# Four edits to the end of a conv-attention, additive-attention and expert kernel: residual and gate loads, the weight buffers, and the last chunk's attention

## The chip, the core and the metric

The kernel runs on one core of one Trainium2 chip. Times are microseconds (us) of the device; the metric is the median of the runs of the whole kernel. Five engines work side by side and wait for one another by semaphores: PE (TensorE, matmuls and transposes), DVE (VectorE), ACT (ScalarE), POOL (GpSimd) and SP (SyncE), which in this kernel issues every DMA.

## What is computed

Eight images of 128 channels and 36 x 36 = 1296 pixels pass through two layers, all in float32.

```
# layer 0, on the group-normed image: 1x1 conv, convolved queries, keys, values, attention, two 1x1 convs
x = x + conv_attention(group_norm(x))
t = tokens(x)                                   # (8, 1296, 128)
# layer 1a: additive attention
y = layer_norm(t);  q = y @ Wq.T + bq;  k = y @ Wk.T + bk
s[b,i,j] = sum_d w[d] * tanh(q[b,i,d] + k[b,j,d]) + bw
t = t + softmax_j(s) @ y
# layer 1b: 64 experts, each takes the 8 tokens of an image with the largest gate
y = layer_norm(t);  p = softmax over the tokens of (y @ gate_w.T + gate_b)     # (8, 1296, 64)
topv, topi = 8 largest of p along the tokens, for each image and expert
pooled[b,e] = sum_k topv * y[topi]
h   = gelu([pooled, 1] @ weight1[e])            # weight1: (64, 129, 512)
out = [h, 1] @ weight2[e]                       # weight2: (64, 513, 128)
t[b, topi] += topv * out[b,e]
```

The sum over tanh for all 1296 x 1296 token pairs of each image is nearly all of the work. The two expert weights are 33.5 MB that have to be read once.

## The kernel before

**The loop over the pairs.** For each image `b` the 1296 queries are cut into three chunks `c` of 432 and the keys into eleven tiles `j`, ten of 128 and a rest of 16. A unit is one (b, c, j), taken in the order j = 0 to 4, 10 (the rest), 5 to 9. The tanh is made of quotients: for each unit twelve slots multiply key features with query features into a denominator `d` and a numerator `n` (PE, line 910), ACT takes the logarithm and then the negative exponential of the denominators (lines 933 and 936), DVE multiplies that with the numerators (958 and 964), and POOL and DVE add up (973, 960). Seven slots after a unit ends, ACT makes its `e`, the exponentials of 128 keys by 432 queries (line 993). When all eleven `e` of a chunk are there, `attend` (lines 715 to 755) multiplies them with the normed tokens: for each of four tiles of 108 queries, eleven matmuls `pa` in two groups of 6 and 5, with a copy `sums` between them (740), then a DVE chain (742 to 750) that divides, adds the token and takes statistics.

**The order of the work.** The program order on each engine is written by hand. Everything beside the pairs is a generator in one of four lanes (`first_of_all`, `urgent`, `gates`, `background`); `take_turns` and `matmul_turn` let them step between the slots, and `matmul_turn` holds the matmuls so added to an average of `PACE` = 400 columns in a slot. `attend` runs in the lane `urgent`, `gating` in the lane `gates`. In the last image there is no next image to prepare.

**The end of the program.** After the last slot the last `e` of the last chunk is made and these follow:

- `attend` of the last chunk, with all 44 matmuls `pa`; then `gate_logits` for it, whose transposes, square root (POOL, 262), gate product `pg` and maximum lead to `gate_tokens` of the last image: softmax (ACT, 830 and 836), the eight largest (DVE, 841), `gt` (844, 846), transposes `tpg` and the 12 products `ppool` that give `pooled` (869). `gt` is written to DRAM as `gd` (847). The sums before the experts, `t2`, lie in DRAM as `t2d` since `gate_logits` (791).
- The buffers of the pair loop are given up (`score.close()`), and the weights take their room: two rings of four buffers of 1 MB, `w1` and `w2`, for groups of four experts. The loads of the first four groups (1123, 1125), of the biases `b1_s` and `b2_s`, then `gd` of the last image stand in SP's queue; behind `pooled` the loads of all gates and residuals (1155, 1157), each for all eight images, and then the other twelve groups of weights, one group for each step of the loop of line 1198.
- That loop has 18 steps for 16 groups: step g runs `outer(g - 2)` (lines 1183 to 1196, 16 matmuls `pout`), `turned(g - 1)` (4 transposes) and `inner(g)` (4 matmuls `phid` with the weights, 4 with the biases, then GELU on ACT). `pooled_s` is a copy of `pooled` with the eight images padded to 32 columns (POOL 1138 and 1139, DVE 1150).
- `out_s` goes to DRAM and comes back turned (1209, 1215); 24 products with the gates (1224) are added to the residuals (DVE, 1227) and written out (1229).

SP runs its queue in order: a DMA whose wait isn't over holds all behind it. Completion is counted on eight semaphores that the DMAs take in turn, and a DMA waits until the one eight places ahead of it in the queue has landed.

Of the kernel before, what the change touches and what calls it, by code (L numbers as in the profile page):

```python
# [70 lines left out]
def kernel(  # L71
# [46 lines left out]
    t2d = [dram.tile([C, N], F32, tag=f"t2d{b}", name=f"t2d{b}") for b in range(NB)]  # L118
    gd = [dram.tile([E, N], F32, tag=f"gd{b}", name=f"gd{b}") for b in range(NB)]

    pooled = const.tile([128, E, NB], F32, tag="pooled", name="pooled")
    ident = const.tile([128, 128], F32, tag="ident", name="ident")
    make_identity(nc, ident)

# [2 lines left out]
    with ExitStack() as loop, ExitStack() as score:  # L127
# [5 lines left out]


        big = pool("big", 8, ctx)
        chunks = pool("chunks", 8)
        etp = pool("etp", NKT + 1)
        one = pool("one", 1)
        two = pool("two", 2)
        kfp = pool("kfp", 3, score, "right")  # L140
# [571 lines left out]

        attended = {}

        def attend(b, c, es):


            xh, _, xr = prepared[b]
            if c == 0:
                t2 = big_tile("t2").rearrange("p (t c) -> p t c", c=128)  # L720
                mv = two.tile([T, NT, 2], F32, tag="t2_mv", name="t2_mv")
                attended[b] = (t2, mv)
            t2, mv = attended[b]
            own = range(c * TPC, (c + 1) * TPC)
            for at in own:
                nc.sync.dma_start(t2[:T, at, :], tokd[b][at * T : (at + 1) * T])
            for i, at in enumerate(own):
                sums = two.tile([T, C + 1], F32, tag="sums", name="sums")
                for some in (range(6), range(6, NKT)):
                    pa = aux("pa1")[:T, : C + 1]  # L730
                    for j in some:
                        if j < NKT - 1:
                            e, v = es[j][:, i * T : (i + 1) * T], xh[:, j, :]
                        else:
                            rows = slice(32 * i, 32 * i + REM)
                            e, v = es[j][rows, :T], xr[rows]
                        bmm(pa, e, v, start=(j == some[0]), stop=(j == some[-1]))
                    yield TAKE
                    if j < NKT - 1:
                        nc.vector.tensor_copy(sums, pa)  # L740
                        yield matmuls()
                nc.vector.tensor_add(pa, pa, sums)
                inv = small.tile([T, 1], F32, tag="inv", name="inv")
                nc.vector.reciprocal(inv, pa[:, C : C + 1])
                nc.vector.scalar_tensor_tensor(
                    t2[:T, at, :], pa[:, :C], inv, t2[:T, at, :], ALU.mult, ALU.add
                )
                st = small.tile([T, 6], F32, tag="t2_st", name="t2_st")
                nc.vector.bn_stats(st, t2[:T, at, :])
                nc.vector.bn_aggr(mv[:, at, :], st)  # L750
                yield matmuls()
            if c == NCH - 1:
                prepared.pop(b)
            if b == NB - 1:
                yield from gate_logits(b, [c])
# [64 lines left out]
        def gate_tokens(b):  # L820
# [48 lines left out]
            nc.vector.tensor_copy(pooled[:, :, b], pp[:, :E])  # L869
            yield matmuls()  # L870

        def drain(*gens):
            for g in gens:
                for _ in g:
                    pass
# [111 lines left out]
        def exps(p, u, d):  # L987
# [4 lines left out]
            e = etp.tile([128, CH], F32, tag="e", name="e")  # L992
            nc.scalar.activation(e[:, : d.shape[-1]], d, AF.Exp, bias=eb_s)  # L993
            es.setdefault((b, c), {})[j] = e
            if len(es[b, c]) == NKT:
                urgent.append(attend(b, c, es.pop((b, c))))

# [74 lines left out]
        for p, (u, k) in enumerate(slots):  # L1072
            b, c, j = units[u]
            rem = j == NKT - 1
            if k == 0:
                prefetch(u + 2)
                if c == 0 and j == 1:
                    if b > 0:
                        gates.append(gating(b - 1))
                    if b + 1 < NB:  # L1080
                        background.extend(
                            (normal(b + 1), conv_keys(b + 1), layer0(b + 1), tokens(b + 1),
# [21 lines left out]
        while pending:  # L1104
# [4 lines left out]


        wts = ctx.enter_context(
            tc.tile_pool(name="wts", bufs=4, side="right", reuse_waits="tile")
        )
        hidp = ctx.enter_context(tc.tile_pool(name="hidp", bufs=2, side="right"))
        biases = ctx.enter_context(tc.tile_pool(name="biases", bufs=1, side="right"))
# [1 line left out]
            tc.tile_pool(name="ps_last", bufs=4, side="right", space=bass.MemoryType.PSUM)  # L1117
        )

        def load_experts(g):  # L1120
            es = slice(g * EG, (g + 1) * EG)
            w1 = wts.tile([128, EG, HID], F32, tag="w1", name="w1")
            nc.sync.dma_start(w1, weight1[es, :128, :].rearrange("e d h -> d e h"))
            w2 = wts.tile([128, EG, NHC * O], F32, tag="w2", name="w2")
            nc.sync.dma_start(
                w2, weight2[es, :HID, :].rearrange("e (p c) o -> p e (c o)", c=NHC)
            )
            return w1, w2

        urgent.run(len(slots))  # L1130
        experts = [load_experts(g) for g in range(4)]
        b1_s = biases.tile([NGR, EG, HID], F32, tag="b1", name="b1_s")
        nc.sync.dma_start(b1_s, weight1[:, 128, :].rearrange("(g q) h -> g q h", q=EG))
        b2_s = biases.tile([128, O], F32, tag="b2", name="b2_s")
        for h in range(2):
            nc.sync.dma_start(b2_s[E * h : E * (h + 1)], weight2[:, HID, :])
        pooled_s = biases.tile([128, E, 32], F32, tag="pooled_s", name="pooled_s")
        nc.gpsimd.memset(pooled_s, 0.0)
        nc.gpsimd.tensor_copy(pooled_s[:, :, : NB - 1], pooled[:, :, : NB - 1])
        drain(*urgent)  # L1140
        drain(gate_tokens(NB - 1))


# [3 lines left out]
    def aux(name):  # L1147
        return ps_last.tile([128, 512], F32, tag="aux", name=name)

    nc.vector.tensor_copy(pooled_s[:, :, NB - 1], pooled[:, :, NB - 1])  # L1150
    gates, res = [], []
    for b in range(NB):
        if b % 2 == 0:
            gates.append(last.tile([128, N], F32, tag=f"gates{b}", name="gates"))
        nc.sync.dma_start(gates[b // 2][E * (b % 2) : E * (b % 2) + E], gd[b])
        res.append(big_tile("res")[:, :N])
        nc.sync.dma_start(res[b], t2d[b])

    out_s = last.tile([128, NGR, O], F32, tag="out_s", name="out_s")
    hidden, hidden_t, sums_of = {}, {}, {}  # L1160

    def inner(g):
        ph = aux("phid")
        for q in range(EG):
            mm(ph[32 * q : 32 * q + 32, :], pooled_s[:, g * EG + q, :], experts[g][0][:, q, :],
               start=True, stop=False)
        of_group = ident[:NGR, g : g + 1].to_broadcast([NGR, 32])
        for q in range(EG):
            mm(ph[32 * q : 32 * q + 32, :], of_group, b1_s[:, q, :], start=False, stop=True)
        x = hidp.tile([128, HID], F32, tag="hid", name="hid")  # L1170
        nc.scalar.activation(x, ph, AF.Gelu)
        hidden[g] = x
# [10 lines left out]
    def outer(g):  # L1183
# [4 lines left out]
        for c in range(NHC):  # L1188
            for q in range(EG):
                mm(po[32 * q : 32 * q + 32, :], xt[:, c, 32 * q : 32 * q + 32],  # L1190
                   experts[g][1][:, q, c * O : (c + 1) * O],
                   start=(c == 0), stop=(c == NHC - 1))
        if g % 4 == 3:
            nc.vector.tensor_copy(
# [3 lines left out]
    for g in range(NGR + 2):  # L1198
# [3 lines left out]
            turned(g - 1)  # L1202
        if g < NGR:
            inner(g)
        if len(experts) < NGR and g >= 2:
            experts.append(load_experts(len(experts)))
    eods = eod.rearrange("b (g q) o -> q b g o", q=EG)
    for q in range(EG):
        nc.sync.dma_start(eods[q], out_s[32 * q : 32 * q + NB])
# [8 lines left out]
    for h in range(NB // 2):  # L1218
        for c in range(NCH):
            cols = slice(c * CH, (c + 1) * CH)  # L1220
            pfs = [aux("pf")[:, :CH] for _ in range(2)]
            for i in range(2):
                half = slice(E * i, E * i + E)
                mm(pfs[i], eos[h][half], gates[h][half, cols], start=True, stop=True)
            for i in range(2):
                r = res[2 * h + i][:, cols]
                nc.vector.tensor_add(r, pfs[i], r)
# [64 lines left out]
```

## Time and profile before

| | |
|---|---|
| median of 3 runs | 6157.78 us (6153.82 to 6159.6) |
| the profiled execution | 6152.63 us |
| its span in the profile | 6150.6 us, mean granted TensorE clock 0.986 |
| PE, PEld, DVE, ACT, POOL busy | 97%, 47%, 78%, 86%, 75% of the span |
| chain that ended last | PE 76%, ACT 8%, DVE 6%, issue 6%, POOL 2%, DMA 1%, SPq 1% |
| last slot's matmuls (PE, line 910) end | 5972.97 us after the span's start |
| first load of expert weights issued | 5974.55 us |
| `pooled` of the last image ready | 6016.16 us |
| last group's outputs in `out_s` | 6119.80 us |

The span runs from the first to the last instruction of the execution. Rows of groups give a line of the kernel, the engine, the operation, what is written from what, how often, and the mean duration; a row of a time window gives for each engine its busy time and its instructions, then the clock granted to TensorE (1.00 is full), the mean busy share of the 16 DMA engines and what they moved in GB/s. "issue" is time in which an engine waited for nothing that the profile shows; SPq is SP at issuing DMAs.

### The profile page before, as it was taken

The numbers are of one execution on the slowest core, as the hardware profiler recorded it, in microseconds if no ns is written. First come the engines' busy times: TensorE is split into PE (matmuls) and PEld (weight loads), VectorE is DVE, ScalarE is ACT, GpSimd is POOL, SyncE is SP. The second block draws the span as 40 slices with busy tenths as digits, with TensorE's granted clock in tenths as the row PEclk, the third lists the DMA queues.
The fourth block names the chain that finished last, engine by engine and source line by source line (L and its number), as shares of the span: only waits on it lengthen the run. The fifth ranks groups of instructions, "written<-read, shape, count | busy, mean of one in ns | idle before, by whom it ended". The sixth has DMA issues, their size and how long they took to land.

```text
span 6150.6 us, 93223 instructions
## 1 busy us (share of the span) xinstructions
PE 5963.4 (97%) x33576; PEld 2866.4 (47%) x33576; DVE 4798.4 (78%) x9518; ACT 5281.1 (86%) x5371; POOL 4597.5 (75%) x2804
## 2 busy tenths in 40 slices
PE   7999999999999999999999999999999999999996
PEld 5454444544544445444445444454454444544443
DVE  4787878878787787877888777887778878788872
ACT  1888898888988899888998899888898888999980
POOL 4777777777778777878687777877777777787870
PEclk9999999999999999999999999999999999999997
DMA  1200011000210001100111001100021000100017
GB/s 47 71 33 22 25 62 52 20 25 28 72 38 24 26 32 64 42 22 23 49 52 37 22 20 63 45 33 22 28 71 39 24 26 27 61 29 29 25 71 262
DMA packets 150239, 270.88 MB, mean 44 GB/s; under 512 B 45392, under 2 KB 74960, under 8 KB 149776
## 3 DMA queue, kind: packets, MB, share of 16 engines
q1 hardware_dynamic: 149776, 264.92, 12.9%
q8 instruction: 265, 4.34, 0.3%
q14 instruction: 198, 1.62, 0.1%
HBM read 200.41 MB, written 64.19 MB: 43 GB/s over the span
## 4 chain that ended last, share of the span: by engine, by line
PE 76%; ACT 8%; DVE 6%; issue 6%; POOL 2%; DMA 1%; SPq 1%; POOLq 0%; DVEq 0%; ACTq 0%
PE n L910 37%; PE d L910 12%; PE pa L281 7%; ACT lq L933 6%; PE pc L281 5%; PE s L281 3%; PE pk L281 3%; PE pq L281 3%; DVE rp L964 2%; DVE n L958 1%; DVE accd L960 1%; PE d L915 1%; ACT lq L936 1%; PE n L915 1%; ACT e L993 1%
## 5 line engine op out<-in xcount | busy, mean ns | idle before, releaser
L973 POOL TENSOR_TENSOR accp<-accp,rp 128x864 f32<-128x864 f32 x1440 | 2917.0, 2026 | 1032.0 <-DVE rp L964 938.9
L910 PE MATMUL n<-qf,kf 32*128 32x432 f32 (+1 forms) x11520 | 3320.8, 573 | 47.6 <-ACT e L993 13.3
L910 PE MATMUL d<-qf,kf 32*128 32x432 f32 (+1 forms) x11520 | 2983.8, 560 | 39.5 <-ACT lq L933 38.9
L933 ACT ACTIVATE lq<-d 128x864 f32<-128x864 f32 x2928 | 2525.3, 879 | 531.2 <-PE d L910 502.6
L964 DVE TENSOR_TENSOR rp<-n,lq 128x432 f32<-128x432 f32 x3912 | 2174.4, 600 | 739.8 <-PE d L910 539.9
L936 ACT ACTIVATE lq<-lq 128x1728 f32<-128x1728 f32 (+1 forms) x1464 | 2398.2, 1638 | 46.3
L910 PEld LDWEIGHTS n<-qf,kf 32*128 32x128 f32 (+1 forms) x11520 | 1207.1, 184 | 1603.2 <-DVE rp L964 584.0
L910 PEld LDWEIGHTS d<-qf,kf 32*128 32x128 f32 (+1 forms) x11520 | 1088.6, 185 | 420.9 <-issue 225.0
L958 DVE TENSOR_TENSOR n<-n,lq 128x432 f32<-128x432 f32 x1440 | 815.2, 608 | 138.7 <-PE n L910 83.7
L960 DVE TENSOR_TENSOR accd<-n,accd 128x432 f32<-128x432 f32 x1440 | 867.4, 602 | 24.7
L971 POOL TENSOR_TENSOR accp<-rp 128x864 f32<-128x864 f32 x240 | 485.5, 2023 | 194.7 <-DVE rp L964 192.0
L708 POOL TENSOR_SCALAR qf<-qf,cs_s 128x432 f32<-128x432 f32 x192 | 261.2, 1366 | 45.1 <-ACT qf L707 44.4
L281 PEld LDWEIGHTS pa<-xh,e 128*108 128x108 f32 x1920 | 226.1, 176 | 123.7 <-DVE rp L964 53.3
L982 POOL TENSOR_TENSOR accd<-accp,accd 128x432 f32<-128x432 f32 x240 | 265.3, 1106 | 18.8
L980 POOL TENSOR_TENSOR accp<-accp 128x432 f32<-128x432 f32 x240 | 264.6, 1103 | 16.7
L281 PE MATMUL pa<-xh,e 128*108 128x129 f32 x1920 | 265.4, 286 | 6.0 <-DVE accd L960 3.1
L281 PE MATMUL s<-q,k 128*116 128x432 f32 x480 | 230.3, 568 | 1.7 <-DVE q L313 1.4
L281 PEld LDWEIGHTS pk<-xT,a_k 128*128 128x128 f32 x1408 | 171.4, 192 | 107.0 <-DVE n L958 33.7
L459 POOL TENSOR_TENSOR tot<-tot,e 116x432 f32<-116x432 f32 x192 | 212.2, 1105 | 6.0 <-ACT e L468 4.6
L468 ACT ACTIVATE e<-s 116x432 f32<-116x432 f32 x240 | 125.0, 521 | 96.7 <-PE s L281 96.3
L281 PE MATMUL pa<-e,vw 116*128 116x432 f32 x480 | 204.6, 549 | 0.0
L281 PE MATMUL pk<-xT,a_k 128*128 128x128 f32 (+1 forms) x1408 | 202.6, 287 | 0.1
(212 smaller groups left out, 3786.5 us busy)
## 6 DMA issues: line engine op xcount, KB each, us to landing
kf<-kd SPq DMA_DIRECT2D x239, 512.0 KB
kd<-ks SPq DMA_DIRECT2D x158, 256.0 KB
w<-in_weight_dram SPq DMA_DIRECT2D x32, 1024.0 KB
wk_t<-wk_t_d SPq DMA_DIRECT2D x7, 768.0 KB
wv_t<-wv_t_d SPq DMA_DIRECT2D x7, 768.0 KB
wq_t<-wq_t_d SPq DMA_DIRECT2D x7, 768.0 KB
x<-in_x_dram SPq DMA_DIRECT2D x8, 648.0 KB
t<-tokd SPq DMA_DIRECT2D x96, 54.0 KB
```

Of the source, the lines that this page charges most:

```text
L281: mm(out, lhsT, rhs, **kw)
L708: nc.gpsimd.tensor_scalar(qf[:, 1, :], qf[:, 0, :], cs_s[:, q : q + 1], None, ALU.mult)
L910: mm(outs[h][:, :CH], kf[rows[h], q, :], qf_of[b, c, q][rows[h], part, :], start=True, stop=True)
L933: nc.scalar.activation(lq[:, o : o + n, :], d[:, :n, :CH], AF.Ln)
L936: nc.scalar.activation(some, some, AF.Exp, scale=-1.0)
L958: mult(ns[h], ns[h], lq[:, o + h, :])
L960: nc.vector.tensor_add(live["d"], ns[h], live["d"])
L964: mult(rp[:, h, :], n, lq[:, o + h, :])
L971: nc.gpsimd.tensor_add(live["p"], live["r"], rp)
L973: nc.gpsimd.tensor_add(live["p"], live["p"], rp)
L980: nc.gpsimd.tensor_add(s[:, 0, :], s[:, 0, :], s[:, 1, :])
L982: nc.gpsimd.tensor_add(d, s[:, 0, :], d)
```

## The change

Four edits, all of them for the last image and the end. First, the residuals of images 0 to 3 are loaded by a generator `residuals(4)`, which stands in the lane `gates` behind `gating(6)`, so during the last image's first chunk. Second, the ring `etp` that holds the `e` is kept to the end of the program; the gates are loaded into twelve of its tiles, in pieces of 64 x 432, those of images 0 to 6 (21 DMAs) and the residual of image 4 ahead of `gate_tokens` of the last image, the rest behind it. Third, the two weight rings become one ring of nine buffers of 1 MB, loaded in the order of use (`w1` of groups 0, 1, 2, then `w2` of 0, `w1` of 3, `w2` of 1 and so on): nine loads at once, one more in each of steps 0 and 1, two in each step from 2 on. `pooled` is kept in a form that the matmuls read in place, and the bias is added by one matmul of 128 columns with a selection `which` that POOL makes, in place of four of 32 columns. Fourth, `attend_early` runs 36 of the last chunk's 44 matmuls `pa` during its last two units, as soon as nine of the eleven `e` are there, and keeps their sums in two tiles; `attend` then has the last two `e` left, 8 matmuls.

In the built program the eight groups of early matmuls stand between the slots of the last unit but one (its last slots) and the last unit (its first nine); up to there PE's order is unchanged. The nine weight loads stand where the eight stood, then the biases, `t2d`, the 21 gates, the residual of image 4, `gd` of the last image, the residuals of 5 to 7, three gates, and 23 weights. The first weight load waits for POOL's last addition but one of the pair loop (before: for a DVE product of the last slot). The residual of image 6 takes the buffer of `gt` and waits for the landing of `gd`.

```diff
+        def attend_early(b, c, es):
+            xh, _, xr = prepared[b]
+            held = [chunk_tile("sums") for _ in range(TPC // 2)]
+            for i in range(TPC):
+                at = (i % 2) * (C + 1)
+                sums = early[i] = held[i // 2][:T, at : at + C + 1]
+                for some in (order[:5], order[6 : NKT - 2] + order[5:6]):
+                    pa = aux("pa1")[:T, : C + 1]
+                    weigh(pa, i, some, es, xh, xr)
+                    yield TAKE
+                    if some[0] == order[0]:
+                        nc.vector.tensor_copy(sums, pa)
+                    else:
+                        nc.vector.tensor_add(sums, pa, sums)
+                    yield matmuls()
...
             for i, at in enumerate(own):
-                sums = two.tile([T, C + 1], F32, tag="sums", name="sums")
-                for some in (range(6), range(6, NKT)):
+                if i in early:
+                    parts, sums = (order[NKT - 2 :],), early[i]
+                else:
+                    parts = (range(6), range(6, NKT))
+                    sums = two.tile([T, C + 1], F32, tag="sums", name="sums")
+                for some in parts:
                     pa = aux("pa1")[:T, : C + 1]
...
+        def residuals(n):
+            for b in range(n):
+                res.append(big_tile("res")[:, :N])
+                nc.sync.dma_start(res[b], t2d[b])
+                yield step()
...
             es.setdefault((b, c), {})[j] = e
+            if (b, c) == (NB - 1, NCH - 1) and len(es[b, c]) == NKT - 2:
+                urgent.append(attend_early(b, c, es[b, c]))
...
                         gates.append(gating(b - 1))
+                    if b == NB - 1:
+                        gates.append(residuals(4))
...
-            tc.tile_pool(name="wts", bufs=4, side="right", reuse_waits="tile")
+            tc.tile_pool(name="wts", bufs=9, side="right", reuse_waits="tile")
...
+        w1s, w2s = {}, {}
+        to_load = deque()
+        for g in range(NGR + 2):
+            if g < NGR:
+                to_load.append((w1s, g))
+            if g >= 2:
+                to_load.append((w2s, g - 2))
+        def load_next():
+            of, g = to_load.popleft()
+            es = slice(g * EG, (g + 1) * EG)
+            of[g] = wts.tile([128, EG, HID], F32, tag="w", name="w")
...
         urgent.run(len(slots))
-        experts = [load_experts(g) for g in range(4)]
+        for _ in range(9):
+            load_next()
...
-        pooled_s = biases.tile([128, E, 32], F32, tag="pooled_s", name="pooled_s")
-        nc.gpsimd.memset(pooled_s, 0.0)
-        nc.gpsimd.tensor_copy(pooled_s[:, :, : NB - 1], pooled[:, :, : NB - 1])
         drain(*urgent)
+        gates = [[etp.tile([128, CH], F32, tag="e", name="gates") for _ in range(NCH)]
+                 for _ in range(NB // 2)]
+        def load_gates(b):
+            half = slice(E * (b % 2), E * (b % 2) + E)
+            for c in range(NCH):
+                nc.sync.dma_start(gates[b // 2][c][half], gd[b][:, c * CH : (c + 1) * CH])
+        for b in range(NB - 1):
+            load_gates(b)
+        res.append(big_tile("res")[:, :N])
+        nc.sync.dma_start(res[4], t2d[4])
         drain(gate_tokens(NB - 1))
...
-    nc.vector.tensor_copy(pooled_s[:, :, NB - 1], pooled[:, :, NB - 1])
-    gates, res = [], []
-    for b in range(NB):
-        if b % 2 == 0:
-            gates.append(last.tile([128, N], F32, tag=f"gates{b}", name="gates"))
-        nc.sync.dma_start(gates[b // 2][E * (b % 2) : E * (b % 2) + E], gd[b])
+    for b in range(len(res), NB):
         res.append(big_tile("res")[:, :N])
         nc.sync.dma_start(res[b], t2d[b])
+    load_gates(NB - 1)
...
         ph = aux("phid")
+        of_group = ident[:E, g * EG : (g + 1) * EG].rearrange("p (q x) -> p q x", x=1)
+        which = hidp.tile([E, EG * 32], F32, tag="which", name="which")
+        nc.gpsimd.tensor_copy(
+            which.rearrange("p (q x) -> p q x", q=EG), of_group.to_broadcast([E, EG, 32])
+        )
+        mm(ph, which, b1_s, start=True, stop=False)
         for q in range(EG):
-            mm(ph[32 * q : 32 * q + 32, :], pooled_s[:, g * EG + q, :], experts[g][0][:, q, :],
-               start=True, stop=False)
-        of_group = ident[:NGR, g : g + 1].to_broadcast([NGR, 32])
-        for q in range(EG):
-            mm(ph[32 * q : 32 * q + 32, :], of_group, b1_s[:, q, :], start=False, stop=True)
+            o = (g * EG + q) * NB
+            mm(ph[32 * q : 32 * q + 32, :], pooled_s[:, o : o + 32], w1s[g][:, q, :],
+               start=False, stop=True)
...
-        if len(experts) < NGR and g >= 2:
-            experts.append(load_experts(len(experts)))
+        for _ in range(min(1 + (g >= 2), len(to_load))):
+            load_next()
```

## The prediction

> **What bounds the kernel now.** I read the table of time windows over the end first, then the chain that ended last, PE's order in time, DVE's order in time, and the windows of the loop around an earlier `attend`. In the windows the last two columns are the DMA engines' busy share and GB/s, the one ahead of them the clock granted to PE.
>
> ```profile
> 5976.00:6000.00 24.00, 18.94 (x90) 14.73 (x88) 8.94 (x31) 0.65 (x1) 5.61 (x6) 0.71 1.02 360
> 6000.00:6017.00 17.00, 7.60 (x41) 6.75 (x44) 7.16 (x12) 4.12 (x4) 0.00 (x0) 0.50 0.11 25
> 6017.00:6044.00 27.00, 19.33 (x176) 6.84 (x168) 2.77 (x4) 2.39 (x4) 0.00 (x0) 0.69 1.01 287
> 6044.00:6110.00 66.00, 49.30 (x576) 22.16 (x580) 9.34 (x14) 6.57 (x11) 0.00 (x0) 0.81 1.04 383
> 6110.00:6120.00 10.00, 8.25 (x84) 3.69 (x76) 1.68 (x3) 0.60 (x1) 0.00 (x0) 0.50 0.05 17
> ```
>
> The end is one long DMA stream with a hole. Eight weight buffers and the biases (8.65 MB) are in by 6000; then the queue is empty for 17 us, as nothing more may be loaded ahead of `pooled`; then 8 MB of gates and residuals at 287 GB/s; then 24 MB of weights at 383 GB/s to 6110. The chain confirms what opens the queue again:
>
> ```profile
> 5978.42 0.66 ACT e L993
> ...
> 6010.47 5.39 PE ppool L281 x24
> 6015.88 0.45 SPq L1155
> ```
>
> PE waits for weights, not the reverse. Its steps are 5.4 us apart, what two weight DMAs take (2 x 1.05 MB at 383 GB/s = 5.5 us):
>
> ```profile
> 6050.13 1.93 PE L1165 MATMUL phid<-w,pooled_s 128*32 128x512 f32 x8 [13.09 <-DMA w<-in_weight_dram]
> ...
> 6098.77 1.08 PE L1165 MATMUL phid<-w,pooled_s 128*32 128x512 f32 x8 [0.44 <-DMA w<-in_weight_dram]
> ...
> 6104.17 1.06 PE L1165 MATMUL phid<-w,pooled_s 128*32 128x512 f32 x8 [1.64 <-DMA w<-in_weight_dram]
> ```
>
> So at the end a byte taken off the stream, or moved into the hole, counts; PE counts after the last arrival only.
>
> **Early attention.** It takes 36 of 44 `pa` from the end into a loop in which PE and ACT are both full. The nearest rows are the units in which image 7's second chunk was attended, beside a plain unit (last):
>
> ```profile
> 5774.53:5800.73 26.20, 26.12 (x174) 15.54 (x170) 22.24 (x51) 20.49 (x20) 17.47 (x10) 1.00 0.07 22
> 5800.73:5821.75 21.02, 20.56 (x117) 10.04 (x118) 20.25 (x44) 20.09 (x20) 17.11 (x11) 1.00 0.10 36
> 5841.70:5861.66 19.96, 19.25 (x98) 7.68 (x96) 16.73 (x31) 19.77 (x21) 16.34 (x10) 1.00 0.08 28
> ...
> 5778.70 1.58 PE L281 MATMUL pa<-xh,e 128*108 128x129 f32 x12
> ```
>
> Six matmuls (twelve records) take 1.58 us, 0.265 each. All of that attention with its gate logits is about 44 x 0.265 + 3 = 14.7 us of PE; the two units grew by 6.24 + 1.06 = 7.3 us, half. The 36 early ones are 9.5 us of PE; half is 4.8. I take a loop longer by **5 us**. Bounds: 0 (all in PE's gaps) and 9.5 (nothing hidden); nothing excludes either, and a gain is excluded, as ACT, PE and DVE lose no work there.
>
> What it returns: behind the last `e` (5979.1) attention now ends with DVE's chain for four query tiles instead of 44 matmuls at a low clock.
>
> ```profile
> 5980.40 0.30 DVE L742 TENSOR_TENSOR pa<-pa,sums 108x129 f32<-108x129 f32 x1 [4.17 <-PE pa L281]
> 5980.73 0.17 DVE L744 RECIPROCAL inv<-pa 108x1 f32<-108x1 f32 x1
> 5980.94 0.35 DVE L745 SCALAR_TENSOR_TENSOR t<-pa,inv,t 108x128 f32<-108x128 f32 x1
> 5981.32 0.29 DVE L749 BATCH_NORM_STATS2 t_st<-t 108x6 f32<-108x128 f32 x1
> 5981.65 0.18 DVE L750 BATCH_NORM_AGGREGATE t_mv<-t_st 108x2 f32<-108x6 f32 x1
> ```
>
> One chain is 1.43 us, four 5.7: done at 5985.4 instead of 5994.6, so `pooled` comes 9.2 earlier, less 5, less the 0.2 us copy of line 1150: first `phid` at 6012.1 (before 6016.5). But the stream starts only when the loop ends, so it starts 5 us later. If the stream has no hole left, the 5 us are paid and the 4.4 us bought lie beside it.
>
> **The stream, piece by piece**, in the profiled execution's clock, L being the loop's 5 us. The first weight waits for POOL's last addition but one (ends 5974.0) and no longer for DVE's product (5974.4): 0.5 us earlier.
> - Nine weights and the biases: 8.65 MB took until 6000; 1.05 MB more at 383 is 2.7: 6002.2 + L. `t2d` of the last chunk, 0.22 MB: 6002.8 + L.
> - 21 gates, 2.32 MB. In the window at 287 GB/s, gates were a third of the bytes. If the residuals moved at 383 like weights, gates moved at 191; I take that: 0.58 us each, 12.2 together. Bounds: full rate, 0.29 (6 us), and below.
> - Residual 4: 1.7. `gd` of the last image (191): 1.7. Residual 5: 1.7: 6020.1 + L. SP stands at residual 6 until `gd` has landed, and behind it stand residual 7, three gates and all 23 weights; [...] I take 2: 6022.1 + L.
> - Residuals 6 and 7: 3.5; three gates 1.7: 6027.3 + L. 23 weights, 24.1 MB: 63.0. The stream ends at 6090.3 + L = **6095.3**, before 6110: 14.7 earlier.
>
> The first four residuals (4 x 1.7 us of DMA, 4 x 0.6 of SP) go to the first chunk of the last image, where the DMA share is near a tenth. The key loads `kf` behind them are issued two units (40 us) ahead of use and SP mostly waits there for PE (line 893: 204.5 us over the last 450), so they cost nothing; with that cover gone, 9 us. POOL's `which` (about 0.3 us) is made up to two steps ahead of the 4 to 6.6 us steps: nothing. POOL loses the two fills of `pooled_s` (2.4 us), after which it idled 13 us: nothing. On SP, `t2d` and the 21 gates stand ahead of `gd`; `t2d` is ready at about 5986 + L, long before the ninth weight, and of those behind `gd` only residual 6 asks for it. The single bias matmul streams as many columns as the four side by side: nothing, either way.
>
> [...] But these DMAs follow each other eight deep; the four 64 KB `eo` loads released DVE at 6128.49, 6129.42 and 6129.98 (two in the first), about 0.45 us apart, SP's spacing of issues. I keep 0.58.
>
> **After the last arrival.** Before, PE had two groups to do at 6104; `out_s` was whole at 6119.8, 9.8 after the stream. In order of use the last three loads are `w2` of 13, 14 and 15, 2.7 us apart. After the first of them come `pout` (1.08), `phT` (0.75), `phid` with bias (2.05), `pout`, `phT`, a copy (0.69), `pout`, a copy: 8.2 at full clock, 13.3 with 1.94, 1.13 and 3.8 at half clock. That is 2.7 to 7.8 after the stream[...]. Which clock?
>
> ```profile
> 6016.50:6030.00 13.50, 12.76 (x80) 3.87 (x80) 1.38 (x2) 1.19 (x2) 0.00 (x0) 0.50 0.97 282
> 6071.00:6095.00 24.00, 17.08 (x227) 7.24 (x225) 4.11 (x6) 2.39 (x4) 0.00 (x0) 0.99 1.05 386
> ```
>
> [...] Here PE was busy 95% of 13.5 us at half clock, and full at 71% busy later. The row decides: neither is sure, I take the middle, 5.2. `out_s` at 6095.3 + 0.9 + 5.2 = 6101.4 instead of 6119.8: **18.4 us earlier**. Behind it nothing changes (30.8 us). Span 6132.2; the execution had 2.0 us beside its span, 6134.2 against its own 6152.6. It lies 5.2 under the median of the runs, 6157.8, on which I put the gain: **6139.4 us**. A measurement tells about 0.2%, 12.3 us, from no change.
>
> **Rivals.**
> - *The loop hides it* (0.13): early attention costs 1 us and gates move at full rate, 4 and 6 less: 6129.4. For: PE has small gaps. Against: the units above grew.
> - *Small gates* (0.12): [...] 6152, no change.
> - *PE becomes the bound* (0.06): all steps at half clock, 6.65 us (6050.13 to 6056.78). From 6012.1, sixteen steps and the last products end at 6124: 6162, 0.07% over the median. It decides from steps of 5.5 us on. For: 6016 to 6030. Against: 0.99 while it waited for weights.
> - *Slower* (0.05): the 24 gates go one at a time, each 0.45 of issue and 1.72 to landing (the chain's `eo`), 2.2 us: 39 us more, 6178. It decides from 1.35 us each (equal) and 1.9 (over 0.2% slower). Against: the `eo` spacing.
>
> **How the numbers follow.** The forecast has 0.64, with its own range 6132 to 6147 from 3.5 to 7 us of loop, 0 to 4 for the `gd` wait and the two clocks. A tenth of it lies above 6145.5, the bound for faster. Faster: 0.56 + 0.13 = 0.69; same: 0.08 + 0.12 + 0.06 = 0.26; slower 0.05. The range 6128.5 to 6154 leaves out the two slowest rivals (0.11) and the edges of the rest.
>
> **What would show it.** The last two units longer by about 5 us together, with ACT's share down. DMA at work through what was 6000 to 6017, with a dent of some 2 us around `gd`. `pooled` about 4 us earlier and without effect. 63 us of weights at 383. After the last load one `pout`. Wrong would be: a hole that stays, gates at over 1 us each, PE steps above 5.5 us without a wait for DMA, or `kf` loads that stop PE in the last image.

## The result and the profile after

The changed kernel takes **6136.92 us** (median of 10 runs, 6133.52 to 6140.74) beside 6152.51 us (10 runs, 6146.83 to 6160.23) for the kernel before in the same rounds: ratio 0.9973, 95% interval 0.9963 to 0.9983, 15.6 us less. The profiled execution took 6140.74 us, its span 6139.0. Lines of the code have moved: 910 to 949, 993 to 1032, 1155 to 1200, 1157 to 1205 and 1217, 1165 to 1234, 1190 to 1256, the loads of weights to 1178 and 1180.

The time windows of the end show that the hole is gone. As before, the last columns are clock, DMA share and GB/s.

```profile
5989.00:6003.00 14.00, 6.89 (x27) 5.20 (x28) 7.55 (x28) 0.65 (x1) 4.12 (x6) 0.62 1.03 383
6003.00:6014.00 11.00, 2.29 (x9) 0.88 (x10) 5.54 (x8) 4.12 (x4) 0.00 (x0) 0.50 1.05 381
6014.00:6028.00 14.00, 13.27 (x52) 7.88 (x54) 2.08 (x4) 0.60 (x1) 0.34 (x2) 0.50 0.65 173
6028.00:6037.00 9.00, 9.00 (x101) 4.30 (x100) 1.38 (x2) 1.20 (x2) 0.81 (x3) 0.88 0.90 307
6037.00:6103.00 66.00, 49.86 (x552) 24.87 (x547) 10.30 (x15) 7.16 (x12) 2.87 (x10) 0.90 1.04 376
6103.00:6110.00 7.00, 3.65 (x77) 2.40 (x76) 1.38 (x2) 0.60 (x1) 0.00 (x0) 0.90 0.07 22
```

Where 25 GB/s were moved for 17 us, the gates now move at 173, behind the weights and ahead of `pooled`, which is ready at 6020.48 (the first `phid`, at 6020.10, is now the product with the bias and needs no `pooled`). The chain of waits shows that the weights set the end:

```profile
6014.79 5.38 PE ppool L284 x24
...
6037.18 7.90 DMA w<-in_weight_dram
...
6047.21 14.99 DMA w<-in_weight_dram
...
6063.95 14.47 DMA w<-in_weight_dram
...
6080.31 14.35 DMA w<-in_weight_dram
...
6107.51 0.70 DVE out_s L1260
```

The chain names `ppool` and `phid` ahead of the load at 6037.18, as a `phid` ends there and frees buffers. They did not hold that load: SP issued the last gates until 6037.08 (34.09 and 2.99 in its row) and the weight 0.1 us behind them. The runs below without early attention and with pairs of gates settle it: one has `phid` 6.6 us later and its second weights at the same place, the other has the same `phid` and its second weights 5.9 us earlier.

In PE's order in time, each step waits 1.6 us for a weight, now ahead of `pout` and not of `phid`. The last three loads are the `w2` of the last three groups; from the first of the three `pout` that use them, at 6100.22, PE works at full clock to the end of the last:

```profile
6078.56 1.08 PE L1256 MATMUL pout<-w,hidT 128*32 128x128 f32 x32 [1.59 <-DMA w<-in_weight_dram]
...
6094.79 1.85 PE L1256 MATMUL pout<-w,hidT 128*32 128x128 f32 x32 [1.60 <-DMA w<-in_weight_dram]
...
6100.22 1.08 PE L1256 MATMUL pout<-w,hidT 128*32 128x128 f32 x32
...
6106.36 1.08 PE L1256 MATMUL pout<-w,hidT 128*32 128x128 f32 x32 [0.79 <-DVE hidT L1246]
```

Of SP's waits, the one for `gd` is there (the columns are us in total, how many waits, the longest):

```profile
SPq L1200 <- DMA w<-in_weight_dram: 6.5, 3, 3.2
SPq L1217 <- DMA gd<-gt: 3.8, 1, 3.8
```

The first row is of gates that stand eight places behind a weight: 6.5 us in three waits. SP issued them at 6009.25, 6011.97 and 6015.61, and those weights had landed at 6009.24, 6011.95 and 6015.60 by their semaphores.

**Two halves with opposite signs.** From the issue of the first weight to the end of the span it was 176.05 us and is 151.62: 24.4 us gained. But the first weight is issued at 5987.38, not at 5974.55: 12.8 us lost. The spans differ by what remains, 11.6. This split, the *loop* up to the first weight load and the *end* behind it, is what the experiments use, since medians of the kernel before lie between 6150.9 and 6154.8 us from one set of rounds to the next, while the end of a profile moves by 1 us, but for stretches of PE at half clock (4 us in the first profile of the kernel before, as shown below).

### The profile page after: what moved, and what is told of

Read it like the earlier page. It is cut to its first block, busy times and chain, and to the rows that moved or that the text cites. A ratio compares the mean times of both kernels' runs of the same rounds, so it can differ in the third digit from the quotient of the medians.

```text
span 6139.0 us, 93072 instructions
## 1 busy us (share of the span) xinstructions
PE 5957.9 (97%) x33480; PEld 2862.1 (47%) x33480; DVE 4796.4 (78%) x9521; ACT 5279.9 (86%) x5371; POOL 4597.7 (75%) x2819
## 4 chain that ended last, share of the span: by engine, by line
PE 77%; ACT 7%; DVE 6%; issue 6%; POOL 2%; DMA 1%; SPq 0%; DVEq 0%; POOLq 0%; ACTq 0%
PE n L949 37%; PE d L949 12%; PE pa L284 7%; PE pc L284 5%; ACT lq L972 5%; PE s L284 3%; PE pk L284 3%; PE pq L284 3%; DVE rp L1003 2%; DVE n L997 1%; DVE accd L999 1%; PE d L954 1%; ACT lq L975 1%; DMA w<-in_weight_dram 1%; PE n L954 1%
## 5 line engine op out<-in xcount | busy, mean ns | idle before, releaser
L949 PE MATMUL n<-qf,kf 32*128 32x432 f32 (+1 forms) x11520 | 3325.3, 574 | 46.5 <-ACT e L1032 13.3
L284 PEld LDWEIGHTS pk<-xT,a_k 128*128 128x128 f32 x1408 | 171.2, 192 | 107.0 <-DVE n L997 33.7
```

The costliest lines, as they stand in the source:

```text
L284: mm(out, lhsT, rhs, **kw)
L949: mm(outs[h][:, :CH], kf[rows[h], q, :], qf_of[b, c, q][rows[h], part, :], start=True, stop=True)
```

## The experiments

The four edits were undone or isolated one at a time, then the two places where the profile after still shows slack were tried. Times are compared as ratios with runs of the kernel before on the same chip. "End" is from the first weight load to the end of the span, "first phid", "second weights" (the first weight load after the eight or nine that are issued at the end of the loop) and "last pout" are counted from the first weight load too. In the changed kernel and all runs made from it the first `phid` is the bias product, 2 us ahead of the first that reads `pooled`. The last column is the time between the last `e` but two and the last but one, in which most of early attention falls.

| run | median us | ratio to before (95%) | first phid | second weights | last pout ends | end | last unit |
|---|---|---|---|---|---|---|---|
| before, profiled | 6152.51 | 1 | 42.0 | 58.8 | 144.5 | 176.05 | 19.95 |
| before again | 6152.03 | 1.0005 (0.9997 to 1.0013) | 42.0 | 58.3 | 140.3 | 171.80 | 19.96 |
| changed | 6136.92 | 0.9973 (0.9963 to 0.9983) | 32.7 | 49.8 | 120.1 | 151.62 | 23.43 |
| no early attention | 6136.62 | 0.9973 (0.9963 to 0.9983) | 39.4 | 50.0 | 121.5 | 153.10 | 19.95 |
| gates in pairs | 6135.64 | 0.9969 (0.9958 to 0.9981) | 32.7 | 43.9 | 114.9 | 146.26 | 23.44 |
| residuals behind | 6146.22 | 0.9986 (0.9979 to 0.9992) | 32.5 | 56.1 | 126.8 | 158.37 | 23.44 |
| old order | 6141.85 | 0.9977 (0.9968 to 0.9985) | 32.7 | 49.3 | 122.3 | 153.49 | 23.44 |
| early alone, on before | 6150.61 | 0.9994 (0.9986 to 1.0002) | 32.7 | 50.1 | 131.4 | 163.21 | 23.44 |
| tail last | 6131.16 | 0.9965 (0.9953 to 0.9978) | 32.7 | 36.7 | 110.0 | 141.40 | 23.44 |
| tail last, no early | 6135.74 | 0.9971 (0.9959 to 0.9982) | 41.8 | 45.8 | 119.9 | 151.48 | 19.95 |
| tail last, narrow pooled | 6123.53 | 0.9952 (0.9939 to 0.9966) | 33.7 | 37.6 | 110.6 | 141.98 | 23.44 |

**Without early attention.** The two lines in `exps` that append `attend_early` are taken out.

> The fourth edit undone, the other three kept. Theory (the stream of loads sets the end, and it starts when the loop ends): the last two units take 20.0 us instead of 23.4 between the e before them and the last e, so the stream starts 3.5 us earlier; pooled comes about 9 us later after the last e (38 instead of 28 us), which stays hidden behind the gates. From the first weight load to the end of the span 151.6 us as before, or up to 2 us more; in all 2 to 3.5 us faster than the changed kernel, about 6134. Rival (early attention pays, because pooled opens the ring of weights): the stretch from the first weight load to the end grows by the 9 us that pooled is later, less 3.5: 5 us slower, about 6142.

Time from first weight to end 153.10, in the profile 1.5 us longer, and the last unit 3.5 us shorter; the medians can't be told apart. `phid` starts 6.6 us later and the second weights at the same place (50.0 and 49.8), so `pooled` lies beside the stream, as the theory has it. The 2 us that its two terms leave are below what the runs can tell.

**The gates of two images in one load.** `gd` of a pair becomes one DRAM tile:

```diff
-        for b in range(NB - 1):
-            load_gates(b)
+        for h in range(NB // 2 - 1):
+            for c in range(NCH):
+                nc.sync.dma_start(gates[h][c], gd_of[h][:, c * CH : (c + 1) * CH])
+        load_gates(NB - 2)
```

> The gates of images 0 to 5 are kept in DRAM two images to a tile and loaded as 128 x 432, nine loads of 221 KB in place of eighteen of 64 x 432; those of images 6 and 7 as before. Theory (loads of 64 partitions move at half rate, 0.65 us each): nine at the full rate are 9 x 0.58 = 5.2 us in place of 18 x 0.655 = 11.8, so the stream ends 6.5 us earlier and from the first weight load to the end it is 145 instead of 151.6 us; about 6130.5. Rival (a fixed price for each load, which grows with the bytes behind it): [...] 2 us gained, about 6135. Rival 2 (something else, pooled or the landing of gd, sets the point from which the last 23 weights load): no gain, 6137.

The end is 5.4 us shorter, near the 6.5 expected; the second weights are issued 5.9 us earlier. SP's queue, of the changed kernel and then of this one:

```profile
6007.70 19.89 SPq L1200 DMA_DIRECT2D gates<-gd  x21
```

```profile
6008.07 11.59 SPq L1206 DMA_DIRECT2D gates<-gd  x9
6019.70 1.73 SPq L1202 DMA_DIRECT2D gates<-gd  x3
```

The first rival (2 us) and the second (none) are both out. Some of the gain is lost again at `gd`, where SP now stands 5.5 us instead of 3.8. The median moved by 1.3 us only, inside the interval.

That the size came out near the theory does not show its reason. This is a window of the changed kernel in which gates alone move, with SP's issues in it:

```profile
6018.00:6027.00 9.00, 8.28 (x27) 3.91 (x26) 0.96 (x2) 0.60 (x1) 0.29 (x1) 0.50 0.60 163
```

```profile
6018.69 2.51 SPq L1200 DMA_DIRECT2D gates<-gd  x4
```

The DMA engines are idle 0.40 of the time, and SP issues without a pause, four loads in 2.51 us, 0.63 each, which is the spacing at which they land there (6018.79 to 6027.67 by their semaphores, fourteen steps of 0.63). With pairs the engines were busy 0.96 of the time at 319 GB/s (6015 to 6021). By the trace's DMA packets, 1728 bytes took a median of 72 ns in the window above. The figures point to SP's issues and not to the DMA engines as the limit of the 64-partition loads, but no run separates the two, and SP issued the first four gates, which stood apart, in 0.44 to 0.45 us each.

**Residuals behind the gates again.** `residuals(4)` is drained behind the gate loads and no longer stands in the last image.

> The first edit undone: the residuals of images 0 to 3 are loaded behind the 21 gates instead of in the last image's first chunk. Theory: 2.65 MB at 383 GB/s are 6.9 us more on the stream, 158.5 from the first weight load to the end, about 6144. Rival: they hide in the time before pooled is there or before gd has landed, 0 to 4 us, 6137 to 6141. If the residual loads in the loop cost the loop something, the last e comes earlier here than in the changed kernel at the same place of the loop from the last image on.

The end is 6.75 us longer, as the bytes have it, and the kernel 9.3 us slower than the changed one, 0.0013 by ratio (8 us). Nothing of it hid. The last image gains nothing from having the four loads away: from its first `e` to the last but two it is 589.8 us here and 589.9 in the changed kernel.

**The old order in the ring of nine.**

```diff
-        for g in range(NGR + 2):
-            if g < NGR:
-                to_load.append((w1s, g))
-            if g >= 2:
-                to_load.append((w2s, g - 2))
+        for g in range(NGR):
+            to_load.append((w1s, g))
+            to_load.append((w2s, g))
...
-        for _ in range(min(1 + (g >= 2), len(to_load))):
+        for _ in range(min(2 * (g >= 2), len(to_load))):
```

> The ring of nine is kept, but loaded in the old order, w1 and w2 of one group side by side, none in steps 0 and 1 and two in each step from 2 on. Theory (order of use leaves one group product behind the last load instead of two groups): out_s is whole about 9.8 us after the stream's end instead of 5.2, 4.6 us slower, about 6141.5. Rival: with PE at full clock behind the last load the two groups take 1 to 2 us more only, 6138.5.

The end is 1.9 us longer, as the rival has it. The median, 4.9 us above the changed kernel's, agrees with the theory; as a ratio it is 0.0004 (2.5 us), and the two intervals overlap, so the end decides. PE's last rows, behind the last wait for a weight:

```profile
6105.43 1.94 PE L1232 MATMUL phid<-w,pooled 128*32 128x512 f32 x8 [1.74 <-DMA w<-in_weight_dram]
6107.14 1.68 PE L1254 MATMUL pout<-w,hidT 128*32 128x128 f32 x32
6108.75 0.75 PE L1242 MATMUL phT<-ident,hid 128*128 128x128 f32 x4
6110.28 1.08 PE L1254 MATMUL pout<-w,hidT 128*32 128x128 f32 x32 [0.78 <-DVE hidT L1244]
```

From there to the end of `pout` it is 5.9 us. In the profile of before the same products, with the bias among them, took 9.4 (6109.59 to 6119.03): these are the 9.8 that the prediction read behind the stream.

**Early attention alone, on the kernel before.**

> The kernel before with the fourth edit alone. Theory: the last two units grow by 3.5 us and pooled comes 9.8 us earlier after the last e; here the queue behind the first weights stands empty until pooled, so all that follows pooled comes 6.3 us earlier: from the last unit but two to the end of the span 6.3 us less, about 6.3 us faster than before. Rival (attention's matmuls cost in the loop what they save at the end): no difference.

Its first `phid` comes at 32.7 instead of 42.0 and the end is 8.6 us shorter than that of the kernel before run again, for 3.5 us of loop: 5.1 gained in the stages. The median is 2.9 us lower, with an interval from 8.6 us less to 1.2 more. The direction is the theory's; the medians alone don't exclude the rival.

**The tail behind the weights.** From the kernel with the gates in pairs; residuals 5 and 6 go between the first weights of steps 0 and 1, and behind the last weight:

```diff
         for _ in range(min(1 + (g >= 2), len(to_load))):
             load_next()
+        if g < 2:
+            load_residual()
+    load_residual()
+    load_gates(NB - 1)
```

> The changed kernel with the gates of image pairs at 128 partitions, and behind the gate write no loads but weights: residuals 5 and 6 one by one between the first weights of steps 0 and 1, residual 7 and the three gates of image 7 behind the last weight, where the products with the gates come 12 us later. Theory (the stream sets the end): the second run of weights starts with the first phid, about 33 us after the first weight load instead of 50, PE releases the first buffers slowly (5.7 us a step at half clock), the last product ends about 108 after the first weight load instead of 120, the span 138 instead of 151.6: about 13 us faster than the changed kernel, 6123. Rival 1: residual 7 and gates 7 now end the chain, no more than 5 us gained. Rival 2 (PE at half clock sets the pace, 6.6 us a step): 18 steps from 33 end at 152 and the time is 6160 or more.

> The same as the run with the tail behind the weights, without early attention. Theory: now the first phid opens the second run of weights, so early attention is worth what it moves pooled: pooled 6.7 us later after the first weight load, the stretch to the end of the span 6 to 7 us longer, the loop 3.5 us shorter, 3 us slower than the run with it. Rival (stream from the loop's end on sets the time): 3.5 us faster than the run with it.

The end fell to 141.4 us, 10.2 less than the changed kernel's (5.4 of it from the pairs), 3.4 short of the expectation. The median fell by 5.8 us only, to 6131.16 where 6123 was expected. The windows of the run with early attention:

```profile
6017.00:6025.00 8.00, 7.76 (x29) 4.41 (x28) 0.27 (x1) 0.17 (x1) 0.29 (x1) 0.50 0.98 279
6025.00:6036.00 11.00, 10.52 (x97) 5.35 (x98) 1.52 (x3) 1.62 (x3) 0.58 (x2) 0.74 0.95 339
6036.00:6090.00 54.00, 43.76 (x512) 21.90 (x515) 10.13 (x15) 6.57 (x11) 3.18 (x11) 0.97 1.04 386
```

The DMA engines are at work nearly all the time (0.95 and more), though at 279 and 339 GB/s in the first two windows. The run's waits show none of PE for the tail loads. Now `phid` opens the second weights, and without early attention the first `phid` comes at 41.8 instead of 32.7 and the end is 10.1 us longer, against 3.5 us of loop: 6.6 in the stages, 4.6 in the medians (whose intervals overlap). The same edit that was worth nothing that can be measured in the changed kernel pays here, because the place of `pooled` has changed from beside the path to on it.

**The drift of the loop.** The last unit explains 3.5 of the 12.8 us. The other 9.95 were there before it, where the order on PE is the same as before. They came in lumps, and the lumps come with the clock. Two units of image 3, of before, then of the changed kernel:

```profile
2412.65:2436.72 24.07, 22.58 (x120) 11.34 (x118) 21.93 (x47) 20.21 (x21) 18.61 (x11) 0.93 0.13 41
2436.72:2458.64 21.92, 21.40 (x116) 10.64 (x116) 21.36 (x45) 20.26 (x20) 16.43 (x10) 1.00 0.07 17
```

```profile
2420.45:2445.81 25.36, 23.86 (x120) 11.07 (x118) 22.02 (x47) 20.20 (x21) 18.57 (x11) 0.87 0.11 39
2445.81:2468.62 22.81, 22.47 (x116) 10.47 (x116) 20.96 (x45) 20.30 (x21) 16.42 (x10) 0.93 0.07 17
```

The same instructions take 1.29 and 0.89 us longer at 0.87 and 0.93 of the clock instead of 0.93 and 1.00. The trace's clock records say what these means are made of: stretches of 3.41 us, or two or three such in a row, at half clock, each worth 1.7 us of clock. Before has one of 3.41 us, in the first of these units, the changed kernel one of 6.83 in the first and one of 3.41 in the second. Over the loop before lost 35.8 us of clock in this way and the changed kernel 51.2. Here and below the loop is counted from the first exponentials of layer 0, some 66 to 69 us after the start, to the last `e` but two. Is that luck, or does the change cause it? Two things of the change touch the loop everywhere: `pooled` is 24 columns wider, with a memset, and `etp` is opened ahead of `chunks`. On the kernel before:

```diff
-    pooled = const.tile([128, E, NB], F32, tag="pooled", name="pooled")
+    pooled_w = const.tile([128, E * NB + 32 - NB], F32, tag="pooled", name="pooled")
+    nc.gpsimd.memset(pooled_w[:, E * NB :], 0.0)
+    pooled = pooled_w[:, : E * NB].rearrange("p (e b) -> p e b", b=NB)
...
-        chunks = pool("chunks", 8)
-        etp = pool("etp", NKT + 1)
+        etp = pool("etp", NKT + 1, ctx)
+        chunks = pool("chunks", 8)
```

> The kernel before with two things of the change that can touch the pair loop alone: pooled widened by 24 columns with its memset, and the ring of the e opened ahead of the ring of the chunks and kept to the end, so that the later tiles lie at other addresses. The end is that of before. Theory (the 10 us by which the last e came later in the one profile of the changed kernel, beyond early attention, were that execution's luck with TensorE's clock): the same time as before, within 2 us, and a profile whose last e lies within 2 us of 5978 plus what the clock lost in the loop. Rival (the layout costs the loop its 6 us in every execution): about 6 us slower than before.

6159.25 us, ratio 1.0010 (1.0002 to 1.0018), 5.7 us: the rival, not the theory. Each half was then tried, beside the unchanged kernel:

> The kernel before once more, unchanged: what two medians of one kernel differ by here (expected within 2 us), and where the last e of a second execution of it lies (5978.4 in the first). If the drift of the loop is luck of an execution, this profile's last e may lie up to 10 us away from the first's, with more or less clock lost in the loop.

> The kernel before with pooled widened by 24 columns and its memset alone. Both together with the other order of the pools cost 5.7 us. Theory [...]: most of the 5.7 us, about 6159. Rival (the order of the pools does it): the time of before, 6153.5.

> The kernel before with the ring of the e opened ahead of the chunks and kept to the end, alone. Theory (the order of the pools does it): about 6159. Rival (the wider pooled does it): 6153.5. If neither run is over 2 us slower, the 5.7 us are not of either part and stay open.

The unchanged kernel came to 6152.03 beside 6150.90 (ratio in the table), the wide `pooled` alone to 6154.04 (1.0006, 0.9997 to 1.0014), the order alone to 6149.30 (0.9999, 0.9991 to 1.0007). The order alone does not do it; the wide tile is likely and not shown by this run, whose interval includes no effect (and whose profile is one of its slowest executions, 6161.01 us). The last test takes the wide tile out of the version with the tail behind the weights; the last group's `phid` then reads the padded copy `rest`:

```diff
-    pooled_s = const.tile([128, E * NB + 32 - NB], F32, tag="pooled", name="pooled")
-    nc.gpsimd.memset(pooled_s[:, E * NB :], 0.0)
+    pooled_s = const.tile([128, E * NB], F32, tag="pooled", name="pooled")
...
+    rest = last.tile([128, EG * NB + 32 - NB], F32, tag="rest", name="rest")
+    nc.gpsimd.memset(rest[:, EG * NB :], 0.0)
+    nc.gpsimd.tensor_copy(rest[:, : EG * NB], pooled_s[:, (E - EG) * NB :])
```

> The run with the tail behind the weights, with pooled at its old width: the last four experts' columns are copied to a padded tile of 56 columns after pooled is there (POOL, beside PE's first step). In the profiles so far nine loops with the wide pooled took 5885.5 to 5892.4 us from the first e to the last but two, four with the narrow one 5880.0 to 5887.7. Theory (the wide tile makes the loop slower): the loop within 5880 to 5888, the time some 5 us under the 6131.2 of the wide one, about 6126, ratio to before near 0.9957. Rival (the clock's luck in each execution): 6131, ratio 0.9965, the loop anywhere from 5880 to 5892. An end of 141.4 us from the first weight load either way.

6123.53 us, 7.6 less than with the wide tile, with an end of 142.0 against 141.4; the intervals of the two ratios overlap (0.9953 to 0.9978, 0.9939 to 0.9966). Its loop took 5880.0 us and lost 35.8 us of clock; the same two units:

```profile
2415.24:2439.29 24.05, 22.56 (x120) 11.42 (x118) 22.00 (x47) 20.21 (x21) 18.61 (x11) 0.93 0.12 41
2439.29:2461.22 21.93, 21.41 (x116) 10.62 (x116) 21.36 (x45) 20.25 (x20) 16.44 (x10) 1.00 0.07 17
```

Over all profiles, five loops with the narrow tile took 5880.0 to 5887.7 us (mean 5883.1) and nine with the wide one 5885.5 to 5892.4 (mean 5890.1). In these two units of image 3 eight of the nine have the changed kernel's two half-clock stretches, the run with the wide tile alone among them, and each of the five has at most the one of before. So the wide tile goes with a slower clock in the loop. Eight of the nine also have the other order of the pools, but so have two of the narrow ones, with loops of 5880.0 us both. The tile is not the whole of it: the two ranges overlap, and single executions of one kernel differ too (5882.1 and 5885.6 for the kernel before). Whether its addresses or its memset at the start do it was not separated. This last kernel is the fastest tried, 0.9952 of before (0.9939 to 0.9966), 13 us under the changed kernel.

## Why the prediction was right, and where its sum was off

The time was forecast at 6139.4 us and is 6136.9; the gain was forecast at 18.4 us and is 15.6. The mechanism was the one that was named: the hole in the stream is filled, the stream sets the end, `pooled` lies beside it. By its own steps:

- *Early attention, 5 us of loop.* It was 3.46 (the last unit 23.43 instead of 19.95, with the same 3.5 in every kernel that has it). `pooled` came 9.1 us earlier after the last `e` (28.7 instead of 37.7; 9.2 forecast) and without effect, as said; taking the edit out left the time as it was.
- *Stream start, 0.5 us earlier.* From 3.87 to 4.44 us ahead of the last `e`: 0.57.
- *Gates, 0.58 each.* They took 0.655 each, 13.75 us for 21 instead of 12.2: 1.5 too little. Joining those of two images took 5.4 us off the end.
- *One bias matmul for four, nothing.* At full clock it took 1.12 us where the four together had taken 1.06, at half clock 2.07 and 1.93; POOL made a `which` in 0.29 us.
- *The wait for `gd`, 2 us.* SP stood 3.8 us; the range ended at 4. Where the queue was empty, the packets of the first weight began 1.07 us after its issue before (issued 5974.55, moving from 5975.62) and 1.09 after (5987.38, 5988.47). The DMA engines were still at 307 GB/s over the 9 us around it (6028 to 6037) instead of 383, so what was lost is about 1.8 us of traffic (an estimate from these rates).
- *The 23 weights, 63.0 us.* They took 63.3. (The 24 MB that the prediction reads up to 6110 are 24 loads of 1.05 MB, 25.2; nothing in the sum rests on it.) The stream ended about 115.6 us after the first weight was issued; the forecast was 116.3. The gates' excess of 1.5 was made up where one piece follows the other, which was not followed further.
- *Residuals moved for nothing.* Moving them back cost 6.75 us of end, and the last image didn't get shorter (589.8 against 589.9 us). The cover held.
- *After the last arrival, 0.9 + 5.2.* The 0.9 was for the landing of the last load, an assumption that no view of before showed. It was 5.2 in all. From the first of the last three `pout` (6100.22) to `out_s` (6108.21) it is 8.0 us, the prediction's sum at full clock (8.2; 13.3 at half); one `pout` ahead of them ran at half clock (1.85). The middle between the two clocks came near because the last load landed (6105.44 by its semaphore) some 2.5 us behind the stream's end and not 0.9: that part is luck.
- *Behind `out_s`, 30.8 unchanged.* 30.8.

The end so came to 151.6 us where these steps say 153.2. Beside early attention, two terms were missing or mis-sized, and in the profile they work against each other:

*The 9.8 us behind the stream in the kernel before.* This was taken as that kernel's own. It was a stretch at half clock. The last products of the kernel before in its first profile, then run again:

```profile
6109.59 1.94 PE L1165 MATMUL phid<-w,pooled_s 128*32 128x512 f32 x8
6111.45 1.93 PE L1169 MATMUL phid<-b_s,ident 16*32 16x512 f32 x8
6113.31 1.94 PE L1190 MATMUL pout<-w,hidT 128*32 128x128 f32 x32
```

```profile
6112.82 1.07 PE L1165 MATMUL phid<-w,pooled_s 128*32 128x512 f32 x8 [1.67 <-DMA w<-in_weight_dram]
6113.82 1.06 PE L1169 MATMUL phid<-b_s,ident 16*32 16x512 f32 x8
6114.81 1.08 PE L1190 MATMUL pout<-w,hidT 128*32 128x128 f32 x32
```

Four executions with that end (run again, wide, order, both) took 171.8 to 172.7 us, not 176.05. Against these the change gained 20.6 us at the end, not 24.4, and the order of use 1.9, not some 4. The row of one execution at half clock stood for the kernel.

*The loop.* The forecast let it grow by early attention only and said that up to there nothing changes, because the order on PE is the same. The 9.95 us of drift were no part of the sum. In medians it is less: 20.6 less the 3.5 of early attention and plus 0.6 for the start is 17.7 us, and 15.6 were gained, which leaves some 2 us. The same account (median gain against what the end, early attention and the start give) leaves 1.5 to 5.5 us for the other eight kernels with the wide tile, 3.3 in the mean of nine, and from 1.4 gained to 2.6 lost for the four with the narrow one. So "`pooled` in a form that the matmuls read in place" was costed at nothing, and the likeliest reading is that it cost some 3 us; the last kernel without it, 7.6 us faster, speaks for more. This part is supported by comparisons, and its mechanism stays open.

*The sum of the misses.* By the prediction's steps the end gains 22.9 us (18.4, plus the 5 of the loop, less the 0.5 of the start); against the four executions it gained 20.6, 2.3 less. Early attention cost 1.5 less than forecast, and the drift took some 2 that were in no step. Together that is the 2.8 us by which the gain fell short. That the total came so near is in part luck, as one miss pays for most of another.

Of the rivals, "the loop hides it" failed at the 3.46 us, "small gates" at the 0.655 us of a gate, "PE becomes the bound" at a step of 5.4 us with 1.6 of waiting (PE's own is 3.6 at full clock, 6100.22 to 6103.84), "slower" at the spacing again.

## What to carry to other kernels

When one long stream of loads sets the end, ask of each edit on which side of the stream's bottleneck it falls: early attention was worth nothing measurable behind a full queue and 5 to 7 us of stages where `pooled` opened the queue. What is needed only after the last load belongs behind it, and a load of 64 partitions took here as long as one of 128 with twice the bytes (0.655 us, and about 0.66 by an estimate from the 5.9 us that pairs saved). And before a duration from one profile enters a sum, look at the clock beside it: a second execution may show the same rows at twice its clock, as the ends of 176.05 and 171.80 us did.

## What the runs showed of the hardware beyond that

- TensorE's clock fell to half for stretches of 3.41 us, or two or three in a row, in a loop with PE busy 97% of the time. How often differed between builds and between two executions of one build: 34 to 51 us of clock lost in fourteen executions, with the loop 5880.0 us long at 34.1 and 35.8 lost, 5885.6 at 42.7, 5892.1 at 51.2. A line through all fourteen gives 0.67 us of loop for 1 us of clock.
- At half clock PE stayed from 6003 to 6028 in the changed kernel although it was busy for 13.3 of the last 14 us: the row has clock 0.50 over the whole of 6014 to 6028.
- Loads of 64 partitions by 1728 bytes took 0.655 us each (13.75 for 21), 169 GB/s; nine loads of 128 partitions in place of eighteen of these brought the second weights forward by 5.9 of 11.8 us, so about 0.66 us (an estimate) moved twice the bytes. SP's issue of the first kind took 0.59 us (median).
